# A gated projection by seven-product blocks: product 0 by its own blocks as well, a pair's matmuls in a given order, and the result's base made in the attention

## Chip, core and metric

The kernel runs on one NeuronCore of a Trainium2 chip. The metric is the device time of one execution in microseconds, the median of several runs; lower is better. The core has a matrix engine (TensorE, PE in the profile; its weight loads are PEld), VectorE (DVE), ScalarE (ACT), GpSimd (POOL) and SyncE (SP, here the main queue that issues DMAs). Matmul results go to PSUM, eight banks of 128 partitions by 512 floats.

## What is computed

A graph network over 1024 nodes of 512 features, with 16384 edges, all in float32:

```python
h = relu(layernorm(x)); x_in = h
h = gcn(batchnorm(h), W_in) + b_in
for i in range(4):
    h = h + attention(ln(h), cond) @ Wo[i]           # 16 graphs of 64 nodes, 8 heads, 256 conditioning rows
    u = ln(h) @ geglu_w[i] + geglu_b[i]               # 512 -> 4096
    val, gate = split(u, 2)
    h = h + (val * gelu(gate)) @ ffo_w[i] + ffo_b[i]  # 2048 -> 512
h = gcn(h, W_out) + b_out
out = x + h + x_in
```

The change sits in `u` and the gate (the gated projection), and in `x + x_in + b_out`, the base to which the last aggregation is added.

## The kernel before

**Seven products.** Nearly every large product is done by a seven-product block scheme: each operand is cut in two by two blocks, sums of blocks are formed on the other engines, and seven block products take the place of eight. The products are numbered so that with u2 = P0 + P5 and u3 = u2 + P6 the four blocks of the result are C11 = P0 + P1, C12 = u2 + P4 + P2, C21 = u3 + P3 and C22 = u3 + P4. P2 and P3 are added in PSUM to what P4 or P6 left there.

**The gated projection.** The 2048 hidden features are worked in slices of 512 (`r` = 0 to 3), each followed by `ffn_out`, which multiplies the slice by its rows of `ffo_w`. In a slice the left operand holds the value and gate weights (`wval`, `wgate` and their sums `ges`), the right one the normalised, transposed nodes (`ln3T` and their sums `ln3S`). C11 and C12 are the value for nodes 0 to 511 and 512 to 1023, C21 and C22 the gate. A `Quad` is one block of 128 features of all seven products, 512 columns wide: a product is two matmuls (two halves of the contraction) of 128x512. Slice 0 runs four quads one after another (`Quad.rest`).

**Pairs.** Slices 1 to 3 run as two `Pair`s, each of the quads `p` and `p + 2`. Here products 5 and 6 are themselves done by seven products of their blocks (`INNER = (5, 6)`, `Pair.seven`, L1010 to L1039): seven matmuls of 128x256 for both quads in place of four of 128x512. They go into the halves of two PSUM banks, `ge` (a, b) and `gf` (c, d). The code gives them in the order 0, 5, 6, 4, then, after a `yield`, 1, 3, 2, each followed by ACT's copy or DVE's add that reads it; the last three add to what is in a, c and d. The document writes these seven matmuls as a, b, c, d, a', c', d'. The sums that the inner scheme needs are made on POOL: of the weights for each slice (`inner_lefts`, into work tiles `gi`), of the nodes once a layer (`inner_right_of`, into `wos`). Products 0, 4, 3, 2 and 1 are whole (`Quad.product`, L918), into the banks `ga`, `gd` and `gc`, and `Quad.end` (L959) makes the gate and the value from them.

**What orders the work.** Each engine has one in-order stream. The framework that records the kernel moves independent instructions within an engine's stream by its own estimate of when they are ready, so the built order differs from the code's; semaphores carry the dependencies between engines. PSUM tiles come from a pool of eight banks, other tiles from pools with fixed numbers of buffers (`work` 10, `accs` 6, `slots` 36).

**The base.** `base_of` (L1392) fetches a block of x again, applies scale, shift and ReLU on ACT, adds `bias_out` and the block on POOL and writes the sum to DRAM. It runs beside the first eight pairs (`beside`, L1419 to L1421). `add_bias` (L1324) adds `ffo_b` to a node block of `h` on POOL; for the last two blocks it stands behind slice 0's gate.

## Time and profile before

| | |
|---|---|
| median of 3 runs | 2511.55 us (2510.85 to 2512.03) |
| the profiled execution, its own time | 2511.2 us |
| its span, first to last instruction | 2509.4 us |
| PE busy | 2487.4 us (99%) |
| DVE / ACT / POOL busy | 1484.3 / 533.1 / 619.8 us (59% / 21% / 25%) |
| granted TensorE clock | 1.0 |
| one pair of a slice (489.0 to 512.2 us) | 23.2 us, PE busy throughout |
| one `ffn_out` of a slice, both halves (535.4 to 559.6 us) | 24.2 us, PE busy throughout |

In a profile line a group of instructions carries its engine, source line, operation, `out<-in` by tile names, its shape (partitions by columns), and `xN` for N records. A float32 matmul of the shapes used here leaves two records, and its end is modelled, so that records of one chain overlap: the distance from start to start is the real pitch. A bracket at the end of a timeline line tells how long that engine was idle before it, and what released it. The list of waits gives engine and line, `<-` the releaser, the total in us, how often, and the longest.

### The profile page before, as it was taken

The numbers are of one execution on the slowest core, as the hardware profiler recorded it, in microseconds if no ns is written. First come the engines' busy times: TensorE is split into PE (matmuls) and PEld (weight loads), VectorE is DVE, ScalarE is ACT, GpSimd is POOL, SyncE is SP. The second block draws the span as 40 slices with busy tenths as digits, with TensorE's granted clock in tenths as the row PEclk, the third lists the DMA queues.
The fourth block names the chain that finished last, engine by engine and source line by source line (L and its number), as shares of the span: only waits on it lengthen the run. The fifth ranks groups of instructions, "written<-read, shape, count | busy, mean of one in ns | idle before, by whom it ended". The sixth has DMA issues, their size and how long they took to land. (4 is left out here: it accounts for less than half of the span.)

```text
span 2509.4 us, 33048 instructions
## 1 busy us (share of the span) xinstructions
PE 2487.4 (99%) x12752; PEld 1820.7 (73%) x12752; DVE 1484.3 (59%) x3265; ACT 533.1 (21%) x1318; POOL 619.8 (25%) x581
## 2 busy tenths in 40 slices
PE   8999999999999999999999999999999999999998
PEld 5778886666678887566687888566677888566665
DVE  9655565566664555666574555655574555665561
ACT  7322222111112222111112222211112222211111
POOL 1322223443220113332420113133401112233300
PEclk9999999999999999999999999999999999999999
DMA  6302232111211112020202222110121111111210
GB/s 180 132 30 93 93 110 68 47 68 34 105 59 61 59 64 68 23 86 17 97 30 76 72 64 59 43 43 26 51 76 59 60 62 65 43 42 51 84 34 34
DMA packets 69380, 161.06 MB, mean 64 GB/s; under 512 B 5768, under 2 KB 6096, under 8 KB 69216
## 3 DMA queue, kind: packets, MB, share of 16 engines
q1 hardware_dynamic: 67120, 153.44, 18.7%
q0 software_dynamic: 1376, 4.30, 0.5%
q8 instruction: 105, 1.72, 0.3%
q10 hardware_dynamic: 720, 1.11, 0.1%
q14 instruction: 59, 0.48, 0.1%
HBM read 135.76 MB, written 23.07 MB: 63 GB/s over the span
## 5 line engine op out<-in xcount | busy, mean ns | idle before, releaser
L302 PE MATMUL ga<-ln3T,wval 128*128 128x512 f32 x512 | 245.6, 593 | 0.0
L302 PEld LDWEIGHTS ga<-ln3T,wval 128*128 128x128 f32 x512 | 96.0, 190 | 89.5 <-issue 85.1
L933 ACT ACTIVATE g<-g,gcols 128x512 f32<-128x512 f32 x128 | 87.3, 716 | 328.8 <-DVE g L946 112.6
L777 ACT ACTIVATE pr<-sc,nmax 128x256 f32<-128x256 f32 x256 | 118.0, 473 | 176.7 <-DVE nmax L772 176.7
L302 PE MATMUL gd<-ln3S,ges 128*128 128x512 f32 x256 | 128.1, 592 | 0.0
L302 PE MATMUL pa_v<-wv,ct 128*128 128x256 f32 x512 | 123.1, 379 | 0.0
L220 POOL TENSOR_TENSOR ges<-wgate,wgate 128x1024 f32<-128x1024 f32 x16 | 37.7, 2353 | 344.3 <-DVE fs L1087 329.1
L302 PE MATMUL fa<-wff,fT 128*128 128x256 f32 x512 | 121.6, 379 | 0.0
L302 PE MATMUL pc_v<-wv,ct 128*128 128x256 f32 x512 | 121.0, 379 | 0.0
L302 PE MATMUL pc_k<-ct,wk 128*128 128x256 f32 x512 | 121.0, 379 | 0.0
L302 PE MATMUL pd_k<-ct,wks 128*128 128x256 f32 x512 | 121.0, 379 | 0.0
L302 PE MATMUL pd_v<-wvs,ct 128*128 128x256 f32 x512 | 120.9, 379 | 0.0
L302 PE MATMUL gd<-ln3T,ges 128*128 128x512 f32 x256 | 120.7, 594 | 0.1
L302 PE MATMUL gc<-ln3S,wgate 128*128 128x512 f32 x256 | 120.3, 592 | 0.0
L302 PE MATMUL pa_k<-ct,wk 128*128 128x256 f32 x480 | 116.2, 385 | 0.0
L302 PEld LDWEIGHTS fa<-wff,fT 128*128 128x128 f32 x512 | 97.3, 190 | 21.8 <-issue 9.1
L302 PEld LDWEIGHTS pc_k<-ct,wk 128*128 128x128 f32 x512 | 97.3, 190 | 13.2
L302 PEld LDWEIGHTS pd_v<-wvs,ct 128*128 128x128 f32 x512 | 97.3, 190 | 13.2
L302 PEld LDWEIGHTS pd_k<-ct,wks 128*128 128x128 f32 x512 | 97.3, 190 | 13.2
L302 PEld LDWEIGHTS pa_v<-wv,ct 128*128 128x128 f32 x512 | 97.1, 190 | 13.5 <-issue 0.4
L302 PEld LDWEIGHTS pc_v<-wv,ct 128*128 128x128 f32 x512 | 95.7, 190 | 12.2
L302 PEld LDWEIGHTS pa_k<-ct,wk 128*128 128x128 f32 x480 | 88.7, 190 | 21.3 <-issue 10.4
(354 smaller groups left out, 4962.3 us busy)
## 6 DMA issues: line engine op xcount, KB each, us to landing
ct<-cond_dram SPq DMA_DIRECT2D x72, 512.0 KB, 4.4
wval<-in_L_gnn_geglu_w_dram SPq DMA_DIRECT2D x32, 512.0 KB, 4.4
wgate<-in_L_gnn_geglu_w_dram SPq DMA_DIRECT2D x32, 512.0 KB, 4.7
wff<-in_L_gnn_ffo_w_dram SPq DMA_DIRECT2D x32, 512.0 KB, 4.0
cond_dram<-ct SPq DMA_DIRECT2D x24, 512.0 KB, 3.0
cond<-in_L_gnn_cond_dram SPq DMA_DIRECT2D x32, 256.0 KB, 4.5
ct<-cond_dram SPq DMA_DIRECT2D x24, 256.0 KB, 5.2
wk<-in_L_gnn_Wk_dram SPq DMA_DIRECT2D x8, 512.0 KB, 5.3
```

The source lines that it names most:

```text
L220: t.tensor_tensor(s1, a21, a22, OP.add)
L302: nc.tensor.matmul(at, left[:, k, l0:l1], right[:, k, r0:r1], start=start and n == 0 and k == 0, stop=n == len(cols_of) - 1 and k == 1, sk ...
L777: nc.scalar.activation(pr3[:, a, :], ps3[:, a, :], AF.Exp, bias=nmax[:, a:a + 1], accum_out=tot[:, a:a + 1])
L933: nc.scalar.activation(pre, pre, AF.Gelu, bias=gcols[:, cg:cg + 1])
```

## The change

- Product 0 is done by seven products of its blocks too (`INNER = (0, 5, 6)`); its node sums get a slot of their own (`gr_l`), its weight sums two more work tiles.
- In a pair, every matmul carries `tc.keep_in_program_order`: PE runs the matmuls of a pair in the order in which the code gives them. Matmuls of other stages may still stand between them.
- A pair's running sums are put into PSUM by ACT copies (P0 into product 0's banks, u2 into those of products 5 and 6 once these are read), and products 4, 3, 2 and 1 are added to them there by the matmuls. `Quad.end` becomes a generator, run for both quads in turn.
- `base_of` moves from the pairs into the attention (groups 1 and 2 of each layer), and its two adds from POOL to DVE; its tiles come from `accs`.
- `add_bias` of the last two blocks moves from behind slice 0's gate to behind the last slice's.

```diff
-        def end(self):
+        def end(self, pa, pc, pd, w7):
             n, c, bias = self.n, self.c, gcols[:, self.cv:self.cv + 1]
-            pc, pd = bank(f"gc_{n}"), self.d
+            def product(i, to):
+                multiply(to, self.left[i], self.right[i], [(c * P, (c + 1) * P, 0, 512)], False,
+                         tc.keep_in_program_order)
+            product(4, pd)
             g1 = t512(f"g1_{n}")
-            nc.vector.tensor_tensor(g1, pd, self.u3, OP.add)
+            nc.vector.tensor_tensor(g1, pd, w7, OP.add)
             self.gate(g1, n)
-            self.product(3, pc, True)
+            yield
+            product(3, pc)
...
-            self.product(2, pd, False)
-            nc.vector.scalar_tensor_tensor(self.u2, pd, bias, self.u2, OP.add, OP.add)
+            product(2, pd)
             f0, f1 = (self.fT[i][c // 2][:, c % 2, :] for i in range(2))
-            nc.vector.tensor_tensor(f1, self.u2, g1, OP.mult)
-            self.product(1, self.a, False)
-            nc.vector.scalar_tensor_tensor(f0, self.a, bias, g0, OP.add, OP.mult)
+            nc.vector.scalar_tensor_tensor(f1, pd, bias, g1, OP.add, OP.mult)
+            yield
+            product(1, pa)
+            nc.vector.scalar_tensor_tensor(f0, pa, bias, g0, OP.add, OP.mult)
+            yield
...
-    INNER = (5, 6)
+    INNER = (0, 5, 6)
...
             def product(k, to, start):
-                nc.tensor.matmul(to, left[k][:, p * P:(p + 1) * P], right[k], start=start,
-                                 stop=True, skip_group_check=True)
+                tc.keep_in_program_order(
+                    nc.tensor.matmul(to, left[k][:, p * P:(p + 1) * P], right[k], start=start,
+                                     stop=True, skip_group_check=True))
...
+        def begin(self, i):
+            steps = self.seven(i)
+            next(steps)
+            return steps, self.banks, self.w
+
         def run(self, sums, beside):
-            q0, q1 = self.quads
-            for q in self.quads:
-                q.a = bank(f"ga_{q.n}")
-            q0.product(0, q0.a, True)
-            steps = self.seven(5)
-            next(steps)
-            q1.product(0, q1.a, True)
-            next(steps)
...
-            q1.product(4, q1.d, True)
-            for q in self.quads:
-                q.end()
+            first, at, w1 = self.begin(0)
+            sixth, dt, u2 = self.begin(5)
+            next(first)
+            for a, w in reversed(list(zip(at, w1))):
+                nc.scalar.copy(a, w)
+            next(sixth)
+            for a, d, u in reversed(list(zip(at, dt, u2))):
+                nc.vector.tensor_tensor(u, a, u, OP.add)
+                nc.scalar.copy(d, u)
+            last, ct, w7 = self.begin(6)
+            next(last)
+            for c, u in reversed(list(zip(ct, u2))):
+                nc.scalar.copy(c, u)
+            for _ in zip(*(q.end(*of) for q, *of in zip(self.quads, at, ct, dt, w7))):
+                pass
+            for q in self.quads:
                 sums(q.c)
             beside(self.p)
...
+        def base_of(nb):
+            xt, xn = fetched.pop(nb), acc_tile(f"again_{nb}")
+            nc.scalar.activation(xn, xt, AF.Relu, bias=x_shift[:, nb:nb + 1],
+                                 scale=x_root[:, nb:nb + 1])
+            nc.vector.tensor_tensor(xt, xt, bias_out, OP.add)
+            nc.vector.tensor_tensor(xt, xt, xn, OP.add)
+            nc.sync.dma_start(base_dram[nb], xt)
...
+                if g in (1, 2):
+                    base_of(2 * l + g - 1)
+
+            if g in (1, 2):
+                fetch_x(2 * l + g - 1)
```

More of the change, by code (lines that the diff above doesn't have):

```diff
@@ L73, in gnn_kernel @@
     hpool = ctx.enter_context(tc.tile_pool(name="hpool", bufs=1))
-    rows = ctx.enter_context(tc.tile_pool(name="rows", bufs=2))
+    rows = ctx.enter_context(tc.tile_pool(name="rows", bufs=1))
     small = ctx.enter_context(tc.tile_pool(name="small", bufs=4))
@@ L111, in load_w, with load_row @@
         return w
-    def load_row(vec, offset, name):
-        t = rows.tile([P, D], F32, tag="row", name=name)
+    def load_row(vec, offset, name, tag="row"):
+        t = rows.tile([P, D], F32, tag=tag, name=name)
         nc.sync.dma_start(
@@ L295, in blocks_of_w, with multiply @@
         return [w[k][:, :, d * M:(d + 1) * M] for d in range(2) for k in range(2)]
-    def multiply(to, left, right, cols_of, start):
+    def multiply(to, left, right, cols_of, start, each=lambda ins: ins):
         for n, (l0, l1, r0, r1) in enumerate(cols_of):
@@ L301, in multiply @@
             for k in range(2):
-                nc.tensor.matmul(at, left[:, k, l0:l1], right[:, k, r0:r1],
-                                 start=start and n == 0 and k == 0,
-                                 stop=n == len(cols_of) - 1 and k == 1, skip_group_check=True)
+                each(nc.tensor.matmul(at, left[:, k, l0:l1], right[:, k, r0:r1],
+                                      start=start and n == 0 and k == 0,
+                                      stop=n == len(cols_of) - 1 and k == 1,
+                                      skip_group_check=True))
     def blocks_out(t):
@@ L957, in rest @@
             return lambda: nc.vector.scalar_tensor_tensor(f0, self.a, bias, g0, OP.add, OP.mult)
-        def end(self):
+        def end(self, pa, pc, pd, w7):
             n, c, bias = self.n, self.c, gcols[:, self.cv:self.cv + 1]
-            pc, pd = bank(f"gc_{n}"), self.d
+            def product(i, to):
+                multiply(to, self.left[i], self.right[i], [(c * P, (c + 1) * P, 0, 512)], False,
+                         tc.keep_in_program_order)
+            product(4, pd)
             g1 = t512(f"g1_{n}")
-            nc.vector.tensor_tensor(g1, pd, self.u3, OP.add)
+            nc.vector.tensor_tensor(g1, pd, w7, OP.add)
             self.gate(g1, n)
-            self.product(3, pc, True)
+            yield
+            product(3, pc)
             g0 = t512(f"g0_{n}")
-            nc.vector.tensor_tensor(g0, pc, self.u3, OP.add)
+            nc.vector.tensor_tensor(g0, pc, w7, OP.add)
             self.gate(g0, n)
-            self.product(2, pd, False)
-            nc.vector.scalar_tensor_tensor(self.u2, pd, bias, self.u2, OP.add, OP.add)
+            yield
+            product(2, pd)
             f0, f1 = (self.fT[i][c // 2][:, c % 2, :] for i in range(2))
-            nc.vector.tensor_tensor(f1, self.u2, g1, OP.mult)
-            self.product(1, self.a, False)
-            nc.vector.scalar_tensor_tensor(f0, self.a, bias, g0, OP.add, OP.mult)
+            nc.vector.scalar_tensor_tensor(f1, pd, bias, g1, OP.add, OP.mult)
+            yield
+            product(1, pa)
+            nc.vector.scalar_tensor_tensor(f0, pa, bias, g0, OP.add, OP.mult)
+            yield
     def inner_left(t, x, s1, s2, s4):
@@ L988, in inner_right @@
         return [b11, b21, b22, t4, t1, t2, t3]
-    INNER = (5, 6)
+    INNER = (0, 5, 6)
     def inner_lefts(l, r, left):
-        rooms = [t512(f"gi_{l}_{r}_{i}") for i in range(3)]
+        rooms = [t512(f"gi_{l}_{r}_{i}") for i in range(5)]
         rooms = [x[:, i * M:(i + 1) * M] for x in rooms for i in range(2)]
@@ L996, in inner_lefts, with inner_right_of @@
                 for n, i in enumerate(INNER)}
-    def inner_right_of(n, right):
-        rooms = [wos[:, 2 * n + k, i * M:(i + 1) * M] for k in range(2) for i in range(2)]
-        return inner_right(nc.gpsimd, right[INNER[n]], *rooms)
+    def inner_right_of(i, right, room):
+        rooms = [room[:, k, j * M:(j + 1) * M] for k in range(2) for j in range(2)]
+        return inner_right(nc.gpsimd, right[i], *rooms)
     class Pair:
@@ L1013, in seven @@
             left, right = (x[i] for x in self.inner)
-            e, f = bank(f"ge_{n}"), bank(f"gf_{n}")
+            e, f = self.banks = bank(f"ge_{n}"), bank(f"gf_{n}")
             a, b, c, d = e[:, :M], e[:, M:], f[:, :M], f[:, M:]
@@ L1039, in seven @@
             yield
+        def begin(self, i):
+            steps = self.seven(i)
+            next(steps)
+            return steps, self.banks, self.w
         def run(self, sums, beside):
-            q0, q1 = self.quads
-            for q in self.quads:
-                q.a = bank(f"ga_{q.n}")
-            q0.product(0, q0.a, True)
-            steps = self.seven(5)
-            next(steps)
-            q1.product(0, q1.a, True)
-            next(steps)
-            for q, w in zip(self.quads, self.w):
-                q.u2 = w
-                nc.vector.tensor_tensor(w, q.a, w, OP.add)
-            steps = self.seven(6)
-            next(steps)
-            for q in self.quads:
-                q.d = bank(f"gd_{q.n}")
-            q0.product(4, q0.d, True)
-            next(steps)
-            for q, w in zip(self.quads, self.w):
-                q.u3 = w
-                nc.vector.tensor_tensor(w, w, q.u2, OP.add)
-            q1.product(4, q1.d, True)
-            for q in self.quads:
-                q.end()
+            first, at, w1 = self.begin(0)
[13 more added lines that the diff above has]
+                pass
+            for q in self.quads:
                 sums(q.c)
@@ L1325, in add_bias, with fetch_x @@
             nc.gpsimd.tensor_tensor(h[nb], h[nb], ffb, OP.add)
+        if l == 0:
+            bias_out = load_row(gcn_out_b, 0, "bias_out", "last")
+            nc.vector.tensor_tensor(x_shift, x_mean.rearrange(
+                "p a (b c) -> p (a b) c", c=2)[:, :, 0], x_root, OP.mult)
+            nc.vector.tensor_scalar(x_shift, x_shift, -1.0, None, OP.mult)
+        fetched = {}
+        def fetch_x(nb):
+            fetched[nb] = acc_tile(f"x_again_{nb}")
+            nc.sync.dma_start(fetched[nb], x[nb * P:(nb + 1) * P, :])
+        def base_of(nb):
[5 more added lines that the diff above has]
+            nc.sync.dma_start(base_dram[nb], xt)
         oTs = []
@@ L1385, in gnn_kernel @@
         kept = slot(f"kept_{l}")
-        fetched, rights = {}, {}
-        def fetch_x(nb):
-            fetched[nb] = t512(f"x_again_{nb}")
-            nc.sync.dma_start(fetched[nb], x[nb * P:(nb + 1) * P, :])
-        def base_of(nb):
-            xt, xn = fetched.pop(nb), t512(f"again_{nb}")
-            nc.scalar.activation(xn, xt, AF.Relu, bias=x_shift[:, nb:nb + 1],
-                                 scale=x_root[:, nb:nb + 1])
-            nc.gpsimd.tensor_tensor(xt, xt, bias_out, OP.add)
-            nc.gpsimd.tensor_tensor(xt, xt, xn, OP.add)
-            nc.sync.dma_start(base_dram[nb], xt)
+        rights = {}
         for r in range(R):
@@ L1411, in gnn_kernel @@
                 fT, fS, quads = pairs_of(l, r, left, right, (lefts, rights))
-                nb = 2 * (l * (R - 1) + r - 1)
-                if nb < NB:
-                    if nb == 0:
-                        bias_out = load_row(gcn_out_b, 0, "bias_out")
-                        nc.gpsimd.tensor_tensor(x_shift, x_mean.rearrange(
-                            "p a (b c) -> p (a b) c", c=2)[:, :, 0], x_root, OP.mult)
-                        nc.gpsimd.tensor_scalar(x_shift, x_shift, -1.0, None, OP.mult)
-                    fetch_x(nb)
-                    fetch_x(nb + 1)
-                    beside = lambda p: base_of(nb + p)
             else:
                 wff = []
+                more = slot(f"gr_{l}")
                 def beside(c):
+                    with waiting_for(quads[c].last, mybir.EngineType.Pool):
+                        if c == 0:
+                            rights[0] = inner_right_of(0, right, more)
+                        elif c < 3:
+                            i = INNER[c]
+                            rights[i] = inner_right_of(i, right, wos[:, 2 * c - 2:2 * c, :])
                     if c == 2:
                         wff.extend(out_weights(nc.vector, l, 0, raw_out))
-                    elif c < 2:
-                        with waiting_for(quads[c].last, mybir.EngineType.Pool):
-                            rights[INNER[c]] = inner_right_of(c, right)
             fT = geglu(quads, fT, fS, not r, beside)
@@ L1437, in gnn_kernel @@
                     lefts = inner_lefts(l, r + 1, left)
-                    if not r:
-                        for nb in range(NB - 2, NB):
-                            add_bias(nb)
                 for s in range(2):
@@ L1448, in gnn_kernel @@
                     projections = load_projections(l + 1)
+                with waiting_for(geglu.last, mybir.EngineType.Pool):
+                    for nb in range(NB - 2, NB):
+                        add_bias(nb)
                 ffn_out(l, r, 0, fT, wff, kept)
```

## The prediction

> **What bounds the kernel now.** I read the page's first part first, then the waits of TensorE, then the timeline of one pair of the gated projection, then the startup, the only place where TensorE (PE) waits.

> ```profile
> PE 2487.4 (99%) x12752; PEld 1820.7 (73%) x12752; DVE 1484.3 (59%) x3265; ACT 533.1 (21%) x1318; POOL 619.8 (25%) x581
> ```
> ```profile
> PE edges L394 <- DVE high L380: 3.8, 1, 3.8
> PE pc L398 <- DMA prow<-in_L_gnn_bn_b_dram: 3.5, 1, 3.5
> PE pa_kT L302 <- DVE v_deg L134: 2.2, 1, 2.2
> ...
> PE pa_kT L302 <- ACT firsts L323: 0.7, 1, 0.7
> ```

> PE is busy 99% of the span, and its longest waits are all at the start or end of the program, none inside the four layers. So a microsecond of matmul saved there is a microsecond saved, and a microsecond for which PE is made to wait is one lost. Whether the change makes it wait is read from one product by seven in the timeline (columns: start, length, engine, line, out<-in, records; a matmul of these shapes leaves two records):

> ```profile
> 490.71 0.59 PE L1021 MATMUL ge<-ln3S,ges 128*128 128x256 f32 x2
> 491.14 0.59 PE L1021 MATMUL gf<-wos,ges 128*128 128x256 f32 x2
> 491.34 0.37 ACT L1025 COPY gt<-ge 128x256 f32<-128x256 f32 x1 [11.92 <-PE ge L1021]
> 491.57 1.02 PE L302 MATMUL ga<-ln3T,wval 128*128 128x512 f32 x2
> ...
> 492.43 0.59 PE L1021 MATMUL ge<-wos,gi 128*128 128x256 f32 x2
> 492.87 1.02 PE L302 MATMUL ga<-ln3T,wval 128*128 128x512 f32 x2
> 493.07 0.42 DVE L1027 TENSOR_TENSOR gt<-ge,gt 128x256 f32<-128x256 f32 x1 [3.18 <-PE ge L1021]
> 493.53 0.42 DVE L1029 TENSOR_TENSOR gt<-gf,gt 128x256 f32<-128x256 f32 x1
> 493.55 0.37 PEld L1021 LDWEIGHTS ge<-ln3S,ges 128*128 128x128 f32 x2 [0.49 <-DVE gt L1027]
> 493.72 0.59 PE L1021 MATMUL ge<-ln3S,ges 128*128 128x256 f32 x2
> 494.15 0.59 PE L1021 MATMUL gf<-wos,gi 128*128 128x256 f32 x2
> ```

> Call the seven matmuls in the code's order a, b, c, d, then a', c', d'; a and b share a bank (`ge`), c and d another (`gf`). The code says a, b, c, d. The engine ran a, c, ga, b, ga, a', d: b stands 1.72 us behind a, with ACT's copy of a between them, and d 1.72 us behind b, with both of VectorE's (DVE's) adds between them. The built program has the reason: b waits for the copy of a, and d for the add that reads c, although each writes the other half of the bank. The whole-width matmuls ga and gd (products 0 and 4) fill these gaps.

> **The change part by part.** *Fewer columns.* Steady pitch is 0.431 us for a 256-column matmul (490.71 to 491.14) and 0.859 us for a 512-column one (491.57 to 492.43). Product 0 of a pair was 4 x 0.859 = 3.44 us and becomes 7 x 0.431 = 3.02: 0.42 saved, in 24 pairs (4 layers, 3 slices, 2 pairs): **-10.0 us**.

> *The given order.* In the built program of the changed kernel, PE's order in a pair is a b c d of product 0, a b c d of product 5, a' c' d' of 0, a' c' d' of 5, all seven of 6, then eight whole-width products of two matmuls. Nothing stands between a and b or between c and d, and the waits are the old ones. So PE, which takes matmuls in order, stands still in each. Prices:
> - From a matmul's start to the start of its reader: 0.63 us (490.71 to ACT's 491.34), 0.64 to DVE (492.43 to 493.07).
> - The readers: ACT's copy 0.37, DVE's add 0.42, the next add 0.46 after the first one's start.
> - Restart of PE after a real wait. Rows of the startup:

> ```profile
> 20.32 1.89 PE L302 MATMUL pa_kT<-ct,wk 128*128 128x256 f32 x8
> ...
> 22.25 0.58 ACT L323 COPY firsts<-pa_kT 128x512 f32<-128x512 f32 x1 [0.17 <-PE pa_kT L302]
> ...
> 22.89 1.99 PE L302 MATMUL pa_kT<-ct,wk 128*128 128x256 f32 x8 [0.68 <-ACT firsts L323]
> ```

> The copy ends at 22.83, PE starts 0.055 later, and its eight records take 0.10 more than the eight before: 0.155. Ends of this cost: 0.055, if only the gap counts, and 0.225 (DVE's add of 493.07 ends at 493.495, the matmul behind it starts at 493.72). I take 0.155, as it is the one row with the same shape and a true stop.

> Four kinds of stop, each less the pitch that it replaces:
> 1. b behind the copy of a: 0.63 + 0.37 + 0.155 = 1.16, less 0.43: 0.73. Three in a pair.
> 2. d behind the second add: from b's start 0.64 + 0.46 + 0.42 + 0.155 = 1.675, less two pitches, 0.86: 0.81. Three.
> 3. d' behind the add that reads c': 0.64 + 0.42 + 0.155 = 1.22, less 0.43: 0.79. Three.
> 4. c' of product 6 behind the add that reads d (in 0 and 5 other matmuls stand between): 1.22 less 0.86: 0.36. One.

> A pair: 2.19 + 2.43 + 2.37 + 0.36 = 7.35 us. The second pair of a slice differs twice. The built order puts two matmuls of `ffn_out` (fa, fc, 0.86 us) between c and d of product 6, which covers a stop of kind 2: -0.81. And on DVE two sums of the first pair (L1097 and L1098 after the change) stand between the first and second add of its product 0. DVE's last `fT` op starts 0.2 after the pair's end and takes 0.75, a sum 0.68 (to 1.63); b begins at 1.16, so the first add runs 1.80 to 2.22, two sums at 0.68 to 3.58, the second add to 4.00, and d starts at 4.16 in place of 1.16 + 1.675 = 2.83: +1.33. A slice costs 7.35 + 7.35 - 0.81 + 1.33 = 15.2, and twelve slices **+182.6 us**. With the restart at its ends (ten stops, 24 pairs) this is 24 less or 17 more.

> *The copies that seed the banks* (six of 128x512 a pair on ACT; the row of the same shape, L926, takes 0.59, so 3.5 us) lie beside the stops and the next matmuls: product 4 needs the bank of product 5, whose copy is done before product 6's d'. Product 3 needs the bank of 6, 3.4 us after product 4 begins; the copy ends 1.7 us after d' starts. They cost nothing, up to 0.6 us (one copy) if that order slips: 14 us at most. DVE loses four ops of 0.69 to 0.75 a pair and gains five of 0.42; it is in no other stop.

> *POOL* gets four more sums of 0.73 a slice in `inner_lefts`. Its work after a geglu is 4 x 2.35 + 12 x 0.7 + 4 x 1.27 = 22.9 us, beside an `ffn_out` of 24.2 us, and the sums that product 0 needs come first: nothing, and 35 us (4 x 0.73 x 12) if that cover were gone. The two `add_bias` (1.26 each) move to the last slice, behind POOL's weight sums of the next layer or, in the last layer, behind its eight `ce` transfers, the last of which went out at 2404.36, 14 us before that pair ended. Who waits for them are DVE's adds into those rows in the second half of `ffn_out`, 12 us later: nothing.

> *`base_of` in the attention.* DVE gets two adds of 0.68 (the nearest SBUF row, L1086) in each of eight key stages, between the second and third add of a product or behind the keys'. Behind them is the add of d, for which PE waits two products of 1.73 us later: covered. If the x block (4.1 us to landing, issued before the keys) is late, DVE and then PE wait: 0 to 2 us each, up to 16 in all; I take 0. On SP the x block needs a free `accs` buffer first, and the next conditioning blocks' loads stand behind it, with a whole stage in hand. The gated slices lose ACT's `again` and POOL's adds, none of them on PE's path: no gain.

> Sum against the profiled execution's own 2511.2 us (span 2509.4, 1.8 outside): 2511.2 - 10.0 + 182.6 = 2683.8. The median of the runs is 0.35 above that execution: **2684 us**.

> **Rivals.** *The order costs nothing* (faster, 0.03): the stops are covered, as in the kernel before, and only the columns count: 2511.5 - 10.0 = 2501.5. For it: PE starts weight loads early (493.55 for 493.72), and these gaps are hidden today. It decides at 0.43 us from a matmul to the matmul behind its reader; the reader's start alone is 0.63. If the stops came to 0.42 us a pair, the change would be worth nothing (0.01).

> *Half the stops* (0.05): the waits overlap more than I think, for instance as a weight load hides the restart and DVE's adds come closer: 90 us, 2593.

> *The clock falls* (0.08). PE works some 9 of the first 16 us of a pair, in pieces of 0.43 to 0.86. If the array were granted half its clock there, 21 matmuls at 0.431 would take 9.05 us more, 217 in all: 2901, and more if it lasts into the whole-width products. For it: the 16 transposes at 10.72 us, after an idle start, take 3.65 us; 16 of the same shape at 18.57 take 1.91. Against it: between 22.89 and 26.59 PE works 1.99 of 3.70 us, and the four matmul records behind take 1.98, their usual 1.88 and the restart's 0.10. [...] The startup's row does not agree, so it keeps a small chance.

> **How the numbers follow.** The main case has 0.83. Its bounds, -24 and +17 for the restart, -16 for DVE's sums if they are moved, +14 and +16 for copies and `base_of`, not all at once, give **2640 to 2725**. The two sides left out, half the stops and faster below, the clock above, have 0.17. A measurement of this kernel can tell about 0.2% (5 us) from no change. Faster 0.03, same 0.01, slower 0.96.

> **What would show it.** Right: a pair takes 30.2 us (22.8 of matmuls and 7.4) where it took 23.2 (489.0 to 512.2); TensorE's waits list, in tens of us each, waits for ACT's copy of a (now L1037) and DVE's adds (L1041, L1043, L1048); PE's share falls to some 94%; matmul durations and granted clock stay. Wrong: PE still at 99% with no such waits (order free), 256-column records at twice 0.38 us (clock), or new PE waits in the attention (`base_of`).

## The result and the profile after

The changed kernel takes 2715.4 us (median of four runs, 2713.8 to 2722.6), the kernel before 2511.5: a ratio of 1.0818 (95% interval 1.0798 to 1.0837), slower, inside the predicted range and 31 us above the predicted value. Its profiled execution is the longest of the four, 2722.6 us with a span of 2720.8 and a mean granted clock of 0.985 (0.988 to 0.989 in the others), so the sum below goes by that one.

The page, busy time of the engine and the granted clock in 40 slices:

```profile
PE 2570.5 (94%) x12896; PEld 1849.6 (68%) x12896; DVE 1485.3 (55%) x3307; ACT 633.4 (23%) x1510; POOL 649.1 (24%) x627
...
PEclk9999999899999999999899999988989999999999
```

TensorE's waits (total us, times, longest):

```profile
PE gf L1033 <- DVE gt L1041: 48.4, 60, 1.7
PE gf L1033 <- DVE gw L1048: 39.4, 72, 0.6
PE ge L1033 <- ACT gt L1037: 36.8, 72, 0.6
```

PE's share fell from 99% to 94%, and the three longest waits now lie inside the gated projection, where there were none. Two details go further than the prediction. The longest wait for L1041 is 1.7 us, where the others are 0.6; and the clock row has slices at 8. And PE's busy time grew by 83 us although it has fewer columns to work, so not all of the loss is waiting.

The timeline of TensorE at the start of a first pair (start, length, [idle before <- releaser]): a, b, c, d of product 0 and a of product 5.

```profile
489.40 0.59 PE L1033 MATMUL ge<-ln3T,wval 128*128 128x256 f32 x2
490.55 0.67 PE L1033 MATMUL ge<-gr,gi 128*128 128x256 f32 x2 [0.55 <-ACT gt L1037]
491.06 0.59 PE L1033 MATMUL gf<-gr,wval 128*128 128x256 f32 x2
492.26 0.70 PE L1033 MATMUL gf<-gr,gi 128*128 128x256 f32 x2 [0.61 <-DVE gt L1041]
492.80 0.59 PE L1033 MATMUL ge<-ln3S,ges 128*128 128x256 f32 x2
```

b starts 1.15 us after a (the prediction says 1.16), behind ACT's copy; d starts 1.71 us after b (predicted 1.675), behind two DVE adds. This pair takes 30.7 us, where it took 23.2.

The same in the second pair of that slice, from b on (b, c and d of product 0, a of product 5):

```profile
521.16 0.70 PE L1033 MATMUL ge<-gr,gi 128*128 128x256 f32 x2 [0.46 <-ACT gt L1037]
521.70 0.59 PE L1033 MATMUL gf<-gr,wval 128*128 128x256 f32 x2
523.91 1.18 PE L1033 MATMUL gf<-gr,gi 128*128 128x256 f32 x2 [1.62 <-DVE gt L1041]
524.88 1.06 PE L1033 MATMUL ge<-ln3S,ges 128*128 128x256 f32 x2
```

And what DVE did meanwhile:

```profile
521.90 0.42 DVE L1039 TENSOR_TENSOR gt<-ge,gt 128x256 f32<-128x256 f32 x1 [0.17 <-PE ge L1033]
522.24 0.68 DVE L1097 TENSOR_TENSOR fs<-fs,fT 128x512 f32<-128x512 f32 x1
522.84 0.68 DVE L1098 TENSOR_TENSOR fs<-fT,fs 128x512 f32<-128x512 f32 x1
523.44 0.42 DVE L1041 TENSOR_TENSOR gt<-gf,gt 128x256 f32<-128x256 f32 x1
```

The two sums of the first pair stand between the two adds, as predicted, and make the stop 1.62 us. Behind it the 256-column records take 1.06 and 1.18 us where they took 0.59 and 0.70, until 541 us, among the matmuls of product 6: the granted clock from 524 to 541 us is 0.50. Of the twelve second pairs six go this way, of the twelve first pairs none.

All 24 pairs of the profiled execution: first pairs take 30.65 to 30.71 us each; second pairs at full clock 31.34 (0.86 of it two matmuls of `ffn_out`); the six at half clock 32.6 to 38.0, together 31.8 us more than six at full clock. Twelve slices of 2 x 23.2 us were 556.9; they are now 368.0 + 376.1 - 10.35 (the `ffn_out` matmuls) at full clock, +176.9 us, and +31.8 for the clock: 208.7 of the 211.4 us by which the span grew. The remaining 2.7 us are found in the last experiment.

### The profile page after: what moved, and what is told of

Its sections match the earlier page's. It is cut to its first block, busy times and chain, and to the rows that moved or that the text cites. A ratio compares the mean times of both kernels' runs of the same rounds, so it can differ in the third digit from the quotient of the medians.

```text
span 2720.8 us, 33750 instructions
## 1 busy us (share of the span) xinstructions
PE 2570.5 (94%) x12896; PEld 1849.6 (68%) x12896; DVE 1485.3 (55%) x3307; ACT 633.4 (23%) x1510; POOL 649.1 (24%) x627
## 5 line engine op out<-in xcount | busy, mean ns | idle before, releaser
L1336 POOL TENSOR_TENSOR hall<-hall,ffb 128x512 f32<-128x512 f32 x32 | 41.1, 1293 | 441.1 <-DVE xn_ln L172 237.7
L1037 ACT COPY gt<-ge 128x256 f32<-128x256 f32 x72 | 26.8, 372 | 456.3 <-PE ge L1033 456.3
L302 PE MATMUL fa<-wff,fT 128*128 128x256 f32 x512 | 124.6, 381 | 0.0
L302 PE MATMUL pa_v<-wv,ct 128*128 128x256 f32 x512 | 123.1, 379 | 0.0
L302 PE MATMUL pc_v<-wv,ct 128*128 128x256 f32 x512 | 121.0, 379 | 0.0
L302 PE MATMUL pd_v<-wvs,ct 128*128 128x256 f32 x512 | 121.0, 379 | 0.0
L302 PE MATMUL pc_k<-ct,wk 128*128 128x256 f32 x512 | 120.9, 379 | 0.0
L302 PE MATMUL pd_k<-ct,wks 128*128 128x256 f32 x512 | 120.9, 379 | 0.0
L302 PE MATMUL pa_k<-ct,wk 128*128 128x256 f32 x480 | 116.2, 385 | 0.0
L302 PEld LDWEIGHTS fa<-wff,fT 128*128 128x128 f32 x512 | 98.3, 192 | 22.3 <-issue 6.7
L302 PEld LDWEIGHTS pd_v<-wvs,ct 128*128 128x128 f32 x512 | 97.3, 190 | 13.2
L302 PEld LDWEIGHTS pd_k<-ct,wks 128*128 128x128 f32 x512 | 97.3, 190 | 13.2
L302 PEld LDWEIGHTS pc_k<-ct,wk 128*128 128x128 f32 x512 | 97.3, 190 | 13.2
L302 PEld LDWEIGHTS pa_v<-wv,ct 128*128 128x128 f32 x512 | 97.1, 190 | 13.5 <-issue 0.4
L302 PEld LDWEIGHTS pc_v<-wv,ct 128*128 128x128 f32 x512 | 95.7, 190 | 12.2
L302 PEld LDWEIGHTS pa_k<-ct,wk 128*128 128x128 f32 x480 | 88.7, 190 | 21.3 <-issue 10.4
L773 DVE TENSOR_REDUCE nmax<-sc 128x2 f32<-128x512 f32 x128 | 82.9, 679 | 10.3 <-PE sc L766 10.3
L849 POOL TENSOR_TENSOR os<-oT 128x256 f32<-128x256 f32 x12 | 8.8, 730 | 317.6 <-DVE oT L824 234.7
L783 DVE TENSOR_SCALAR pr<-pr,inv 128x256 f32<-128x256 f32 x256 | 82.2, 363 | 2.9
```

The lines of the kernel that those rows point to most:

```text
L302: each(nc.tensor.matmul(at, left[:, k, l0:l1], right[:, k, r0:r1], start=start and n == 0 and k == 0, stop=n == len(cols_of) - 1 and k == ...
L773: nc.vector.tensor_reduce(nmax, ps3, AX.X, OP.max, negate=True)
L783: scores.last = nc.vector.tensor_scalar(pr3[:, a, :], pr3[:, a, :], inv[:, a:a + 1], None, OP.mult)
L849: t.tensor_tensor(s1, a21, a22, OP.add)
L1037: nc.scalar.copy(s1, a)
L1336: nc.gpsimd.tensor_tensor(h[nb], h[nb], ffb, OP.add)
```

## The experiments

The theory after the result: the given order makes PE stand behind each reader (some 180 us), and the one long stop in the second pairs drops the clock (some 30). Rivals: the scheme itself (three products by seven, seeded banks) is slow whatever the order; the moved work (`base_of`, `add_bias`) costs something; the clock falls for another reason.

**The order freed.** The changed kernel, without its pinned order.

```diff
-                multiply(to, self.left[i], ..., False, tc.keep_in_program_order)
+                multiply(to, self.left[i], ..., False, lambda ins: ins)
...
-                tc.keep_in_program_order(nc.tensor.matmul(to, left[k]..., right[k], ...))
+                nc.tensor.matmul(to, left[k]..., right[k], ...)
```

> The changed kernel without the pinned order: the framework may move a pair's matmuls again, all else stays (product 0 by seven, seeded banks, base in the attention). Theory 'order' (PE stops behind the readers of a bank because nothing stands between the matmuls): most stops go. In the built order about two of kind 3 and 4 are left in a pair (c', d' of product 5 one behind the other), 1.6 us x 24 = 38, less 10.0 for the columns: 2540 us, 2501 to 2560, clock 1.0. Rival 'scheme' (the third product by seven and the seeding copies give ACT and DVE too much to do, whatever the order): 2650 us or more.

Measured: 2569.6 us, ratio 1.0232 (1.0215 to 1.0249), granted clock 0.999. Freeing the order brings back 146 of the 204 us (the clock's part, some 24, among them), so most of the loss is the order. The value expected was missed by 30 us, and the time lies between the ranges of theory and rival; the waits of TensorE say where:

```profile
PE gf L1032 <- DVE gw L1047: 12.4, 24, 0.5
PE gf L1032 <- DVE gw L1042: 12.4, 24, 0.5
```

The order that results puts d, c' and d' of product 5 one behind another with nothing between them:

```profile
496.79 0.59 PE L1032 MATMUL gf<-wos,gi 128*128 128x256 f32 x2
497.90 0.70 PE L1032 MATMUL gf<-wos,ges 128*128 128x256 f32 x2 [0.52 <-DVE gw L1042]
499.12 0.70 PE L1032 MATMUL gf<-ln3S,gi 128*128 128x256 f32 x2 [0.52 <-DVE gw L1047]
```

So two stops of 0.52 us of idle, each with its restart, stay in every pair, and the second pairs have more (at 519.98, 521.20 and 522.41 us of the first slice). So in this kernel the order that the framework finds does not fill the gaps, as it did in the kernel before with whole-width matmuls of products 0 and 4; that their absence is the reason is not shown. Whether the scheme could be fed at all was left open by this run.

**The order alone.** The kernel before, with the matmuls of its pairs pinned in the code's order and nothing else changed.

```diff
+                tc.keep_in_program_order(
+                    nc.tensor.matmul(to, left[k][:, p * P:(p + 1) * P], right[k], ...))
...
+                q.each = tc.keep_in_program_order     # whole-width products of a pair
```

> The kernel before with one edit: the matmuls of a pair are pinned to the order in which its code gives them. Products 0 and 4 stay whole and stand between some of the steps. Theory 'order': products 5 and 6 each stop PE once by kind 1, 2 and 3, with the lengths seen in the changed kernel 0.80 + 0.88 + 0.82 = 2.5 us, 5.0 a pair, 120 in all: 2631 us, 2610 to 2650, no loss of clock, since 1.7 us of whole matmuls stand ahead of each pair's first step. Rival 'scheme': 2511 us, within 5.

Measured: 2628.4 us, ratio 1.0468 (1.0450 to 1.0485), clock 1.0. 117 us in 24 pairs are 4.9 us a pair. TensorE's waits are those of kinds 1, 2 and 3, 48 times each. The prediction's terms for them are 2 x (0.73 + 0.81 + 0.79) = 4.7; kind 4 is not there, as product 4 stands between d and c' of product 6. The order costs this in a kernel that has none of the change's other parts.

**The moves alone.** The kernel before, with only `base_of` in the attention and `add_bias` in the last slice, as in the change.

```diff
-            nc.gpsimd.tensor_tensor(xt, xt, bias_out, OP.add)      # in the gated slices
+            nc.vector.tensor_tensor(xt, xt, bias_out, OP.add)      # in the key stages
...
+                if g in (1, 2):
+                    base_of(2 * l + g - 1)
```

> The kernel before with only the moves: the base made in the attention with its adds on DVE, and the last two bias adds moved to the last slice. Theory 'nothing': 2511 us within 3, PE waits as before. Rival 'late x block': each of eight places makes DVE and then PE wait up to 2 us: up to 2528 us, with PE waits behind DVE's c22 adds of the keys.

Measured: 2511.1 against 2511.2 us, ratio 0.9999 (0.9989 to 1.0009). Nothing, as predicted.

**The long stop taken away.** The changed kernel, with the three sums of the first pair's second quad on POOL in place of DVE, in the gated slices with pairs.

```diff
             else:
-                nc.vector.tensor_tensor(s2, a22, a21, OP.subtract)
+                t = nc.gpsimd if c == 2 and not begun else nc.vector
+                t.tensor_tensor(s2, a22, a21, OP.subtract)
...
```

> The changed kernel with the three sums after quad 2 of slices 1 to 3 (L1096 to L1098) on POOL in place of DVE, so that they no longer stand between the two first adds of the second pair. Theory 'one long stop drops the clock': the stop of 1.62 us ahead of d shrinks to 0.6, second pairs take 30.0 us, none of them at half clock: 16 us for the stop and about 24 for the clock off 2715: 2675 us, 2665 to 2685, clock 1.0. Rival 'many short stops drop the clock': 16 us off and half the second pairs still slow: 2699 us, clock 0.988.

Measured: 2679.9 us, ratio 1.0671 (1.0654 to 1.0689), clock 0.999, and not one record of a pair at half clock. Second pairs take 30.34 us (one 30.71), first ones are unchanged (one is 31.01). Of the 35.5 us won, 12 x (31.34 - 30.34) = 12.0 are the stop itself and the rest (some 24) is the clock. Taking away the stop took away the clock loss.

**Longer stops put in.** The kernel with the sums on POOL, and l + 1 extra DVE ops between the two adds of product 0 in layer l, in all pairs.

```diff
             nc.vector.tensor_tensor(u2, b, s1, OP.add)
+            for _ in range(int(self.n[0]) + 1 if i == 0 else 0):
+                nc.vector.tensor_tensor(u2, u2, u2, OP.max)
```

> The changed kernel with the three sums of the pair's second row block on POOL (so that no pair loses its clock), and with one, two, three or four extra DVE ops (a maximum of u2 with itself, 128x256, in place, which changes no value) between the two first adds of product 0, in both pairs of each slice: one in layer 0, two in layer 1, three in layer 2, four in layer 3. Nothing else on PE or DVE changes. The stop in front of d of product 0 is 0.61 us of idle without them and was 1.62 in the second pairs of the changed kernel. At about 0.46 us an op the four doses are 1.07, 1.53, 1.99 and 2.45 us of idle, 27.6 us in all (6 pairs a dose). Theory 'a long stop drops the clock': from about 1.5 us on, 256-column records of 1.06 to 1.22 us follow in about half of the pairs, in first pairs as in second ones, none at 1.07; at some 5 us a pair this is 45 us more: 2679.9 + 27.6 + 45 = 2753 (2725 to 2800). Rival 'it was something else in the second pair' (the sums on DVE, the work before it): no record at half clock anywhere, and 2679.9 + 27.6 = 2707.5 (2700 to 2715).

Measured: 2847.9 us (2843.0 to 2857.8), ratio 1.1355 (1.1338 to 1.1373), clock 0.943. The rival is out, since first pairs lose their clock too. The size was missed: 19 of 24 pairs have records at half clock, where half were expected. In the timeline, d and the next a of a first pair in layer 1 (two ops) and in layer 2 (three):

```profile
1239.99 0.70 PE L1033 MATMUL gf<-gr,gi 128*128 128x256 f32 x2 [1.53 <-DVE gt L1043]
1240.53 0.59 PE L1033 MATMUL ge<-ln3S,ges 128*128 128x256 f32 x2
...
1894.90 1.22 PE L1033 MATMUL gf<-gr,gi 128*128 128x256 f32 x2 [1.99 <-DVE gt L1043]
1895.92 1.06 PE L1033 MATMUL ge<-ln3S,ges 128*128 128x256 f32 x2
```

In first pairs, stops of 1.07 and 1.53 us of idle (two pairs each) left the clock alone, and 1.99 to 3.16 us dropped it in all eight, for 16 to 18 of their 21 matmuls. In second pairs two of three with 1.44 to 1.46 us lost it, and all nine with longer stops did, four of these for only two to six matmuls. So the length of the stop alone does not tell them apart; the last section has PE's busy time ahead of each fall of the clock in the changed kernel. (The first pair of each layer has a stop 0.7 to 1.0 us longer than its dose; in layer 0 the first of the new ops took 1.43 us.) The span is 162.5 us above that of the kernel with the sums on POOL; the waits for the second add are 78.9 us in place of 37.6, so 41 us are the stops and 121 the clock.

**Another filler.** The kernel with the sums on POOL, and c ahead of b in each product by seven.

```diff
+            product(6, c, True)
             product(5, b, False)
             nc.vector.tensor_tensor(u2, b, s1, OP.add)
-            product(6, c, True)
```

> The changed kernel with the sums of the second row block on POOL, and one edit to the given order: c of each product by seven is issued ahead of b (a c b d in place of a b c d), 72 times. Theory 'a chain': the start of d is set by a, copy, b, add, add, whatever stands between a and b; c fills 0.43 us of the stop in front of b and takes them from in front of d, so the pair stays at 30.7 us: 2679.9 (2675 to 2690), with the stop in front of b down from 0.55 to some 0.1 us and the one in front of d up from 0.61 to some 1.05 us. Rival 'each filler saves its own length': 72 x 0.43 = 31 us less, 2649 (2640 to 2660). If stops of 1.05 us drop the clock, both come some tens of us later, with 256-column records above 1 us.

Measured: 2675.4 us, ratio 1.0653 (1.0635 to 1.0671), clock 0.999; 4.5 us less, not 31. In most places the stop in front of b went from 0.55 us to 0.18 or less, that in front of d from 0.61 to 0.98. Within one product by seven a, copy, b, add, add, d is a chain, and a matmul put into it moves a stop and doesn't shorten the chain. Stops of 0.98 us didn't drop the clock in any pair.

**The order by hand.** Three chains can fill each other's gaps. The change's scheme, with its three products by seven interleaved so that each matmul starts at least three pitches of 0.43 us ahead of the one behind its reader, the whole-width products in the order 1, 4, 3, 2, and all of it still pinned; s1 and u2 live in the result tiles, since three products need six of these at once; product 0 is added from its SBUF tile; the first pair's sums go to POOL.

```diff
-            first, at, w1 = self.begin(0)
-            sixth, dt, u2 = self.begin(5)
-            next(first)
...
+            for step in ("0a 0c 5a 5c 0b 6a 5b 6c 0d 6b 0A 0C 5d 5A 6d 0D 5C 6C 6A 5D 6D").split():
+                steps[int(step[0])][step[1]]()      # A, C, D: a', c', d'
...
             f0, f1 = (self.fT[i][c // 2][:, c % 2, :] for i in range(2))
+            product(1, pa)
+            yield
             product(4, pd)
```

> The change's scheme (products 0, 5 and 6 by seven, the other four onto banks seeded by copies) with another given order: the three sevens of a pair are interleaved, 0a 0c 5a 5c 0b 6a 5b 6c 0d 6b 0a' 0c' 5d 5a' 6d 0d' 5c' 6c' 6a' 5d' 6d', so that at least three 0.43 us matmuls lie from a matmul to the one that waits for its reader (1.06 to 1.2 us are needed); then whole-width products in the order 1, 4, 3, 2. s1 and u2 live in the tiles of the results, as six result tiles are needed at once; u5 takes product 0 from its SBUF tile; the sums of the first pair go to POOL. Theory 'the order alone makes the stops': they are gone but for 0 to 0.5 us a pair, PE is at 98 to 99%, and the fewer columns show: 2501.5 + 24 x 0.25 = 2507 (2500 to 2520), ratio 0.998. Rival 'three sevens of short matmuls can't be fed' (DVE has 15 adds of 0.42 to 0.46 us in the 9.05 us of a pair's sevens, ACT six copies behind them): stops of 1 to 3 us a pair stay, in front of the last d' and of product 1: 2525 to 2575.

Measured: 2505.0 us, ratio 0.9977 (0.9968 to 0.9986), clock 0.999. PE is back at 99%, and none of its longest waits lies in a pair:

```profile
PE 2479.6 (99%) x12896; PEld 1848.3 (74%) x12896; DVE 1445.6 (58%) x3259; ACT 632.6 (25%) x1510; POOL 712.0 (28%) x675
```

A pair takes 22.80 us (490.62 to 513.42 in the first slice), which is its matmuls and nothing else (21 x 0.431 + 16 x 0.859); in 24 pairs that is 9.7 us less than in the kernel before. So neither the scheme nor the pinning is slow; this one order was.

**The same with the sums on DVE.**

```diff
-                t = nc.gpsimd if c == 0 and not begun else nc.vector
+                t = nc.vector
...
-                t = nc.gpsimd if c == 2 and not begun else nc.vector
+                t = nc.vector
```

> The kernel of the hand order, with all sums of fT back on DVE, as in the changed kernel. In the hand order's trace DVE ends the last fT op 0.95 us after the second pair begins and its first add of product 0 could start at 2.36 us; four sums of 0.68 in between push that add to 3.7 us, so d of product 0 (due at 3.46 us) waits for two adds until 4.6: about 1.2 us in each of twelve slices. Theory 'DVE's queue sets the start of the second pair': 2505 + 14 = 2519 (2512 to 2528), one wait of some 1.2 us for DVE in each second pair and none elsewhere. Rival 'the sums did not matter once the sevens are interleaved' (they are put elsewhere in DVE's order): 2505 (2502 to 2508). No clock loss by either, since PE has four or more matmuls on both sides of the stop.

Measured: 2510.6 us, ratio 0.9999 (0.9989 to 1.0008): 5.6 us more than with the sums on POOL, where 14 were expected, and between the two ranges. The direction holds: DVE's four sums push the first add to 3.5 us into the second pair, and d of product 0 waits for L1042, 12 times. But the wait is 0.18 us and not 1.2, because two matmuls of `ffn_out` (0.86 us), which no order pins, came in just ahead of it. The expectation had overlooked this filler, which the prediction had used.

**The last 2.7 us.** Both the changed kernel and the one ordered by hand have two new waits in the first slice of a layer, which has no pairs. TensorE, DVE and POOL of the kernel ordered by hand there:

```profile
462.73 1.98 PE L302 MATMUL gc<-ln3S,wgate 128*128 128x512 f32 x4 [0.25 <-DVE gu L944]
465.06 1.98 PE L302 MATMUL gd<-ln3T,ges 128*128 128x512 f32 x4 [0.35 <-DVE g L947]
```
```profile
460.86 1.21 DVE L215 TENSOR_TENSOR wffs<-wff,wffs 128x512 f32<-128x512 f32 x1
...
463.19 1.21 DVE L1106 TENSOR_TENSOR fs<-fT,fT 128x512 f32<-128x512 f32 x1
```
```profile
459.22 2.30 POOL L997 TENSOR_TENSOR wos<-ln3T 128x256 f32<-128x256 f32 x2 [6.32 <-DVE fT L958]
461.48 2.37 POOL L997 TENSOR_TENSOR wos<-ln3T,wos 128x256 f32<-128x256 f32 x2
```

Two DVE ops with both inputs in SBUF take 1.21 us, where they took 0.68 before, beside four POOL sums that take some 1.2 us each, where the same shape takes 0.73 elsewhere. Those are the block sums for product 6; in the kernel before there was no third set, and POOL was idle here. The edit puts them one quarter earlier:

```diff
-                        elif c < 3:
-                            i = INNER[c]
-                            rights[i] = inner_right_of(i, right, wos[:, 2 * c - 2:2 * c, :])
+                        elif c == 1:
+                            for j, i in enumerate(INNER[1:]):
+                                rights[i] = inner_right_of(i, right, wos[:, 2 * j:2 * j + 2, :])
```

> The kernel of the hand order, with the block sums of the right side of product 6 (four sums on POOL a layer) made in the second quarter of the first slice, straight behind those of product 5, instead of in the third quarter. In the hand order's trace POOL runs them at 459.2 to 463.8 us, and two of DVE's sums beside them, L215 and L1106, take 1.21 us where they took 0.68 in the kernel before; DVE then comes late to gc and gd and PE waits twice a layer, 2.4 us in all and eight restarts of 0.155. Theory 'DVE and POOL are in each other's way there': those two DVE ops are back at 0.68, the waits for gc and gd are gone, and the time is 2505.0 - 3.6 = 2501.4 (2500.5 to 2503). Rival 'DVE is late for another reason': 2505.0 (2504 to 2506) with the same waits. A third outcome is that the collision moves to the second quarter, with waits there: 2503 to 2507.

Measured: 2501.8 us, ratio 0.9963 (0.9949 to 0.9976), and both waits are gone; DVE's op is at its old length:

```profile
460.92 0.68 DVE L215 TENSOR_TENSOR wffs<-wff,wffs 128x512 f32<-128x512 f32 x1
```

This version beats both kernels, and it is within 0.3 us of what the prediction's first rival gives for fewer columns without stops (2501.5).

## Why the prediction was right, and where its steps were off

*Fewer columns, -10.0 us: right.* Shown by the pair of 22.80 us in place of 23.2, and by 8.9 us between the kernel before and the last experiment.

*The given order: right in mechanism, some 7% short in size.* The waits are those named, for L1037, L1041, L1043 and L1048. A first pair was to take 30.2 us and takes 30.7: the ten stops are 7.9 us and not 7.35, 0.055 us more each. The term that was mis-sized is the restart: 0.21 us and not 0.155, close to the upper end of 0.225 that the prediction gave from DVE's row. It was put once into each stop, and the rows show it twice: a matmul that starts behind a true wait is longer (0.67 to 0.70 for 0.59), so the next matmul starts 0.51 to 0.54 us behind it in place of 0.43, and where it has a reader on the chain, that one starts later too (DVE 0.71 us behind b, at 491.26, in place of 0.64).

*The second pair: right.* Predicted 30.15 - 0.81 + 1.33 + 0.86 = 31.5 us with the two `ffn_out` matmuls, measured 31.34 at full clock. Both corrections, fa and fc as fillers and the two DVE sums between the adds, are there in the trace.

*The clock: wrong as a whole or nothing.* The prediction gave it 0.08, for all 21 matmuls of all pairs (217 us). What came was a part: six second pairs, 31.8 us in the profiled execution. The step that failed is the reading of the row set against it: 1.99 us of work in 3.70 had not dropped the clock, so no pair was to. This is the row in the kernel before:

```profile
26.59 1.98 PE L462 MATMUL hw_in<-w_in,h0T 128*128 128x512 f32 x4 [1.71 <-ACT h0T L454]
```

Its stop is longer than the 1.62 us, so it is not the length that sets the two apart. The work around the stops differs: PE was busy for 1.99 and 2.91 us of the two stretches of 3.41 us over which this stop lies (22.67 to 29.50), and for 1.33 us of the 3.41 ahead of the fall at 523.98 in the changed kernel (last section). In the second pair, whose stop the prediction had worked out (its +1.33), three matmuls, 1.3 us by their pitch, lie in the 3.8 us from its start to d. The price of the wait was summed, and the work left around it not held against the row. How often PE stops was not enough for a fall: with the sums on POOL each pair has nine or ten stops, the longest two of all at 0.97 and 0.98 us and the others at most 0.62, and not one record of a pair is at half clock.

*The moves, the seeding copies and `inner_lefts` at nothing: right.* The moves alone are 0.9999; six copies a pair cost nothing in a pair of 22.80 us (the order by hand).

*POOL: one step was not listed.* The third set of right-hand block sums in the first slice was left out, as POOL had room there. It had, but DVE had none to give: 2.4 us of waits and eight restarts, 3.3 us by the last experiment. By itself it is inside the 0.2% that this kernel's measurement can tell.

*The sum.* 2683.8 predicted for the profiled execution; +31.8 for the clock, +3.3 for POOL's sums and +4.1 for the longer stops (12 x 0.53 less 12 x 0.19) give 2723.0, measured 2722.6. Most of the 31 us by which the median lies above the value is the clock, and without it the time would have been inside the range too.

## What to carry to other kernels

A chain of matmul, reader and matmul on one bank, given in program order, kept its length here when a matmul was put into it (4.5 us won with c ahead of b, where 31 would have been each filler's own length); count how many independent chains are needed to cover it (here three, with three pitches of 0.43 us over each gap of 1.1 to 1.2) before the order is pinned. When a wait is costed, the work that is left around the longest single stop is to be held against the clock too (here 1.24 to 1.64 us in the 3.41 ahead of each fall), and not only the sum of the stops. Work put on an idle engine is not free for that alone: here four POOL sums stood beside DVE ops of 1.21 us in place of 0.68.

## What the runs showed of the hardware

```profile
520.57:523.98 3.41, 1.33 (x6) 0.75 (x5) 3.11 (x6) 0.37 (x1) 0.00 (x0) 1.00 0.00 0
523.98:527.39 3.41, 2.95 (x6) 1.90 (x7) 0.42 (x1) 0.37 (x1) 0.00 (x0) 0.50 0.00 0
```
```profile
1240.78:1244.20 3.42, 1.67 (x7) 0.81 (x5) 2.39 (x5) 0.09 (x1) 0.00 (x0) 1.00 0.00 0
1244.20:1247.61 3.41, 2.46 (x10) 1.73 (x10) 1.27 (x3) 0.44 (x2) 0.00 (x0) 1.00 0.00 0
```

Leaving out the first 20 and the last 40 us, PE is busy for 1.24 to 1.64 us in the six steps ahead of a fall, and for at least 1.67 us in the 748 steps at full clock that have no fall behind them. In the kernel before, which has no fall there, the emptiest of 716 such steps has 1.97 us (84.11 to 87.52). In the twelve second pairs of the changed kernel, with nearly the same stop, the emptiest step holds 1.24 to 1.64 us in the six that lost their clock and 1.67 to 2.07 in the six that did not. So which six it was goes with where the steps lay over the stop. At the place of the startup's row the step has 1.99 us of work in the kernel before (22.67 to 26.08), where the stop is 1.7 us long; in the moves alone and in the order by hand the stop there is 2.2 us long, and the mean granted clock of the first 100 us is 0.98 in place of 1.00. This was read from the traces afterwards, and no run was made to test it. What brings the clock back is not settled.

DVE and POOL were slower beside each other: in the kernel ordered by hand 1.21 us in place of 0.68 on the one side, some 1.2 in place of 0.73 on the other, and with POOL's sums one quarter earlier the DVE op was back at 0.68. Both of the stretched ops read two tiles in SBUF (L215 at 460.86 and L1106 at 463.19); two others that do so beside the same POOL sums (L214 at 460.26 and L216 at 462.59) kept their 0.68 us. Why two were stretched and two not was not shown.
